# Two dot products of a graph kernel's tail: summed on ScalarE instead of VectorE

## The chip, the cores and the metric

The kernel runs on one core of a Trainium2 chip. A core has TensorE (PE: matrix products into PSUM), VectorE (DVE), ScalarE (ACT: functions of one operand, with an optional running sum of what it writes), GpSimd (POOL) and SyncE (SP, which here issues the DMAs between device memory and SBUF). Each engine works through its own queue in order and waits on semaphores for the others. The metric is the device time of one execution in microseconds; lower is better.

## The reference, cut to what matters

There are 32 graphs of 512 nodes with 64 features. Four layers follow each other, each with a residual and a norm over the features: a degree-normalised product with the adjacency matrix, a Chebyshev convolution of order 4, an attention in hyperbolic space (logarithm map, sigmoid attention, exponential map, projection), and an aggregation by weighted quantiles over a thinned neighbourhood, with a small two-layer network behind it. The change touches the end of the third layer. There the sum over neighbours becomes the tangent vector `u` of each node, and this is mapped back to the ball:

```python
def mobius_add(x, y, c):
    x2 = jnp.sum(x * x, axis=-1, keepdims=True)
    y2 = jnp.sum(y * y, axis=-1, keepdims=True)
    xy = jnp.sum(x * y, axis=-1, keepdims=True)
    num = (1.0 + 2.0 * c * xy + c * y2) * x + (1.0 - c * x2) * y
    den = 1.0 + 2.0 * c * xy + c * c * x2 * y2
    return num / jnp.maximum(den, MIN_NORM)
...
support_t = jnp.einsum('bij,bijd->bid', att, x_local)
support_t = jnp.clip(support_t, -CLAMP, CLAMP)
return proj(expmap(support_t, x, c), c)
```

The kernel never forms the pairwise vectors. It needs two dot products per node over the 64 features: of `x` with the weighted sum `S` of the neighbours (for the coefficient of `x` in `u`), and of `u` with `x` (the `xy` of the Moebius sum).

## The kernel before

A graph is a batch. Its 512 nodes lie as 128 partitions by T = 4 groups, a node's 64 features along the free dimension, so a `wide` tile is 128x4x64 and a `col` tile, one number per node, 128x4. Each batch passes through stages that the code calls lanes:

- `front` (L1000) loads the adjacency matrix and the features and does the first two layers. Its result, with some columns of scalars, goes to `FLS` (L1564), a tile with two halves: batch b uses half b % 2 (L1076).
- `pairs` (L1086) forms the 512x512 attention in float32 on TensorE, ScalarE and VectorE, and ends in `SS`, the weighted sums, copied from PSUM.
- `tail` (from L1211, still in that function) is the mapping back. The first dot product (`q`, tile `tail_xs`, L1215) enters `s1`; `v = x * s1` and `u = S * hb - v` follow, clipped. Then come the square sum `un` (L1224) and the second dot product `ux` (L1225). A long run of 128x4 operations, mostly on GpSimd, with one tanh on ScalarE, turns `un` and `ux` into two coefficients; `ux` is first read at L1238, after the tanh. The last reader of the batch's half of `FLS` is `scaled(v, x2, al)` (L1259). A layer norm gives `x3`.
- `graph` thins the neighbourhood and ranks the nodes by neighbour count. `gather` (L1270) selects neighbours by one-hot products on TensorE, into the strips `SB` and `SH`. `sort` (L1368) and `head` (L1399, once for two batches) run sorting networks of VectorE minima and maxima over them and weigh the quantiles (`sort_prod`, `PRS`). `finish` and `dense` (L1444 on) do the small network and store the result.

`rowsum` (L847) is used for the two dot products alone. It multiplies on VectorE into the tile `pr` and sums with one reduction of 128x256 to 128x4. `square` (L855) does its sums otherwise: four ScalarE activations of 128x64, one for each group, that write a throwaway tile `junk` (one buffer for each lane) and accumulate into one column of the result. The hardware executes each of these as an ACTIVATE and an ACTIVATION_READ_ACCUMULATOR.

What sets the order is a planner, the class `Order`. While the lanes are called, batch by batch, `op` (L289) only records each operation with its engine, an assumed issue time, an assumed latency and its dependences. `issue` (L361) then lays all operations of all batches out over five simulated queues and emits them in that order, which the hardware queues keep. Two things steer it:

- due times: `due` (L334) gives every operation a time, period x (batch + a number from `STAGES`), the number read off the lane's list of five knots by how deep the operation lies in its lane. The period is 80. Of the operations that are ready on an engine the planner takes the one with the earliest due time.
- margins: `after` (L354) says when a result can be used. On another engine that is the end plus the latency plus `HOP` (0.05) plus `LATE` (0.08).

Where the planner sees TensorE idle for more than 0.3, it puts in fillers (L453), products that keep the engine active: on zeros, or, while no accumulation is open, on constants.

Of the kernel before, what the change touches and what calls it, by code (L numbers as in the profile page):

```python
# [8 lines left out]
F32 = mybir.dt.float32  # L9
# [5 lines left out]
AF = mybir.ActivationFunctionType  # L15
OP = mybir.AluOpType
# [4 lines left out]
P = 128  # L21
# [218 lines left out]
class Order:  # L240
# [3 lines left out]

    ENGINES = ("PE", "DVE", "ACT", "POOL", "SP")
    HOP = 0.05
    LATE = 0.08
    STAY = 58.8

    def __init__(self, nc, tc):  # L250
# [103 lines left out]
    def after(self, d, i, end, full):  # L354

        a, b = self.ops[d], self.ops[i]
        if a[0] == b[0]:
            return end + (a[2] if full and a[0] != "PE" else 0.0)
        return end + a[2] + self.HOP + self.LATE

# [109 lines left out]
def tile_adj_resnorm(ctx: ExitStack, tc: tile.TileContext, x, adj, nodemask, w1k, b1k, att_w, att_b,  # L470
                     w1, b1, w2, b2, out):
    nc = tc.nc
    B, N, D = x.shape
    T = N // P
# [12 lines left out]
    pools = {}  # L487
# [3 lines left out]
    seq = Order(nc, tc)  # L491

    def width(a):
        n = 1
        for d in a.ap[1:]:
            n *= d[1]
        return n

    def vec(f, out, ins, one=False, scalars=(), reads=None, **kw):

        n = width(reads if reads is not None else out)
        tiles = [out] + list(ins)
        rate = 1.04e-3
        if not any(a.space == PSUM for a in tiles):
            half = all(a.dtype in (F16, BF16) for a in tiles)
            if one:
                rate = 0.26e-3 if half else 0.52e-3
            elif half:
                rate = 0.52e-3
        sc = [a for a in scalars if isinstance(a, bass.AP)]  # L510
        seq.op("DVE", 0.07 + n * rate + 0.065 * len(sc), 0.085, f, [out], list(ins) + sc)

    def tt(out, a, b, op):
        vec(lambda: nc.vector.tensor_tensor(out, a, b, op=op), out, [a, b])  # L514
# [14 lines left out]
    def reduce(out, a, op):  # L529
        vec(lambda: nc.vector.tensor_reduce(out, a, axis=AX.X, op=op), out, [a], reads=a)  # L530
# [12 lines left out]
    def act(out, a, f, bias=None, scale=1.0, accum_out=None, after=None):  # L543
        sc = [x for x in (bias, scale) if isinstance(x, bass.AP)]
        kw = {k: v for k, v in (("bias", bias), ("accum_out", accum_out)) if v is not None}
        n = width(out)
        table = "exp" if f in (AF.Ln, AF.Exp) else "sig" if f in (AF.Sigmoid, AF.Tanh) else None
        near = 0.06 if a.space == PSUM else 0.1
        seq.op("ACT", near + n * 0.83e-3 + 0.09 * len(sc) + (0.09 if accum_out is not None else 0.0),
             0.1, lambda: nc.scalar.activation(out, a, f, scale=scale, **kw), [out, accum_out], [a, after] + sc, table)  # L550
# [247 lines left out]
    def col(name):  # L798
        return seq.tile(pools["small"], [P, T], F32, name, 2)

    def wide(name, tag=None):
        return seq.tile(pools["small"], [P, T, D], F32, name, 1, tag)
# [44 lines left out]
    def rowsum(a, b, name):  # L847

        pr = wide("pr")
        tt(pr, a, b, op=OP.mult)  # L850
        s = col(name)
        reduce(s, pr, OP.add)
        return s

    def square(a, name):  # L855
# [230 lines left out]
    def pairs(b, res):  # L1086
# [126 lines left out]
        s1 = col("s1")  # L1213
        gtt(s1, SS[:, :, D], SS[:, :, D + 1], op=OP.add)
        q = rowsum(x2, S, "xs")  # L1215
        stt(s1, q, -2.0, s1, op0=OP.mult, op1=OP.add)
        tt(s1, s1, hh, op=OP.mult)
# [5 lines left out]
        ts(u, u, 1e6, -1e6, op0=OP.min, op1=OP.max)  # L1223
        un = square(u, "un")  # L1224
        ux = rowsum(u, x2, "ux")  # L1225
        uc = col("uc")
        gts(uc, un, TINY * TINY, None, op0=OP.max)
# [277 lines left out]
    def within_bounds():  # L1505

        gm, BT = pools["gm"], B * T
        seq.lane = "graph"
        p1, p2, p3 = bank(), bank(), bank()
        ge = [seq.tile(gm, [P, T, N], F16, "ge", 1, t).rearrange("p t n -> p (t n)") for t in ("nbT", "v")]  # L1510
        ge = [ge[s % 2][:, s // 2 * BT:(s // 2 + 1) * BT] for s in range(K + 1)]
        seq.lane = "check"
        m = M3.rearrange("p b t -> p (b t)")

        for s in range(K + 1):
            ts(ge[s], m, float(s), None, op0=OP.is_gt)
        for s in range(K + 1):
            mm(p1[:BT, s:s + 1], ge[s], onesP[:, 0:1], start=True, stop=True)
        cs = seq.tile(gm, [BT, K + 1], F16, "cs")
        act(cs, p1[:BT, :K + 1], AF.Copy)  # L1520
        mm(p2[:B, :K + 1], graphs[:BT, :], cs, start=True, stop=True)
        off = seq.tile(gm, [B, 2, K + 1], F16, "off")
        for i, op in enumerate((OP.is_gt, OP.is_lt)):
            tt(off[:, i, :], p2[:B, :K + 1], limits[:, i, :], op=op)
        bad = seq.tile(gm, [B, 1], F32, "bad")
        reduce(bad, off.rearrange("p i s -> p (i s)"), OP.max)
        badh = seq.tile(gm, [B, 1], F16, "badh")
        cp(badh, bad)
        mm(p3[:1, 0:1], badh, onesP[:B, 0:1], start=True, stop=True)
        ts(flag, p3[:1, 0:1], 0.0, None, op0=OP.is_gt)  # L1530
# [2 lines left out]

    STAGES = {"front": (-0.67, -0.59, -0.59, -0.4, -0.35), "pairs": (1.01, 1.02, 1.54, 1.44, 1.34),
              "tail": (2.23, 2.13, 2.56, 2.68, 2.58), "graph": (0.84, 1.06, 1.03, 1.48, 2.2),
              "gather": (2.92, 2.89, 2.92, 3.03, 2.93), "sort": (4.18, 4.47, 4.53, 5.09, 6.03),
              "head": (4.54, 5.59, 5.59, 6, 7.54), "ends": (4.04, 4.143, 4.245, 4.348, 4.45),
              "check": (1.75, 1.83, 1.91, 1.99, 2.07)}  # L1540

# [1 line left out]
    with ExitStack() as fast:  # L1543
# [59 lines left out]
        within_bounds()  # L1603
        seq.issue(80.0, STAGES, stay_active, 0.3)
        seq.lane = "dense"
# [141 lines left out]
    with tc.If(flagv > 0):  # L1747
        with ExitStack() as slow:
# [24 lines left out]
            for h in range(4):  # L1773
                t = cst.tile([P, T, QC * ROWS], BF16, name=f"parts{h}")
# [32 lines left out]
def build(inputs):  # L1807
    import numpy as np
    import concourse.bacc as bacc

    nc = bacc.Bacc("TRN2", target_bir_lowering=False, num_devices=1)
    arrays, args = {}, []
    for name in _INS:
        a = np.ascontiguousarray(inputs[name])
        if a.dtype == np.bool_:
            a = a.view(np.uint8)
        arrays[f"in_{name}_dram"] = a
        args.append(nc.dram_tensor(f"in_{name}_dram", a.shape, mybir.dt.from_np(a.dtype), kind="ExternalInput").ap())
    args.append(nc.dram_tensor("out_0_dram", inputs["x"].shape, F32, kind="ExternalOutput").ap())
    with tile.TileContext(nc) as tc:  # L1820
        tile_adj_resnorm(tc, *args)
    return nc, arrays
# [8 lines left out]
```

## Time and profile before

| | us |
|---|---|
| median of 3 runs | 2337.36 (2331.5 to 2339.77) |
| the profiled execution | 2326.41 |
| its span, first to last instruction | 2324.6 |
| reductions of the two dot products (`tail_xs`, `tail_ux`) on VectorE | 64, 13.1 + 13.1 busy |
| products before them (`tail_pr`) on VectorE | 64, 13.3 + 13.3 busy |
| accumulating squares of the tail (`tail_junk<-tail_u`) on ScalarE | 128, 33.9 busy, and 26.4 for the accumulator reads |
| table loads on ScalarE | 126 profiled, 1.283 each |

The busy time of an engine counts each moment once. In a group of instructions, though, the single times are added, and neighbours on VectorE and ScalarE overlap: the next one starts before the one before it has ended. What an instruction costs its engine is therefore read from the distance between two starts. A busy TensorE is not TensorE at its peak. The profile names instructions by the tile that is written, with the lane in front: `tail_junk<-tail_u` is the square of `u` in the lane `tail`. As helpers record all operations, many instructions share one line (L514 for all products of two tensors, L550 for all activations), and the tiles tell them apart.

### The profile page before, as it was taken

To read this page: it belongs to the slowest core of one execution; us is meant where nothing else is said; L and a number is where in the kernel's file an instruction comes from. 1 tells how busy PE (TensorE), PEld (TensorE's weight loads), DVE (VectorE), ACT (ScalarE), POOL (GpSimd) and SP (SyncE) were. 2 spreads that over 40 slices of the span, in tenths; PEclk is the share of its full clock that TensorE was granted. 3 is DMA by queue.
4 is the path that set the end of the run, shared out by engine and by line. 5 is a ranking of instruction groups with operands and counts; after the bars stand their busy time and mean duration, and the time that the engine had idled before them with its cause. 6 is when DMAs were issued, how large, how long until landed. Compare 5 with 4: busy or idle time off the path is not lost. (4 is left out here: it accounts for less than half of the span.)

```text
span 2324.6 us, 53396 instructions
## 1 busy us (share of the span) xinstructions
PE 2177.0 (94%) x18555; PEld 1504.3 (65%) x18555; DVE 2115.8 (91%) x6952; ACT 2033.9 (87%) x5818; POOL 1098.7 (47%) x2256
## 2 busy tenths in 40 slices
PE   6999999999999999999999999999999999999987
PEld 4666666666666666666666666666666666666655
DVE  4556999999999999999999999999999999999996
ACT  6798989999998989898989989898998989899753
POOL 1133445545464544545445554544555454454431
PEclk9999999999999999999999999999999999999999
DMA  1010001111000110100011111001111000100000
GB/s 45 21 42 12 18 22 31 27 28 31 27 18 21 34 28 26 33 26 20 22 31 28 27 33 26 19 21 32 29 27 33 26 19 17 29 15 8 13 15 14
DMA packets 131716, 57.72 MB, mean 25 GB/s; under 512 B 56140, under 2 KB 129516, under 8 KB 131436
## 3 DMA queue, kind: packets, MB, share of 16 engines
q1 hardware_dynamic: 126432, 50.09, 8.0%
q0 software_dynamic: 3840, 3.94, 0.8%
q8 instruction: 148, 2.42, 0.4%
q14 instruction: 132, 1.08, 0.2%
q10 hardware_dynamic: 1164, 0.18, 0.0%
HBM read 41.86 MB, written 12.32 MB: 23 GB/s over the span
## 5 line engine op out<-in xcount | busy, mean ns | idle before, releaser
L514 DVE TENSOR_TENSOR SB<-SB 128x92 f32<-128x92 f32 (+12 forms) x1312 | 555.3, 448 | 15.3 <-ACT SB L550 6.2
L569 PE MATMUL gather_bank<-gather_oh,tail_x3h 128*64 128x256 f16 (+5 forms) x5376 | 496.5, 318 | 7.4 <-ACT SB L550 7.1
L569 PEld LDWEIGHTS <-tail_x3h 128*64 128x64 bf16 x5376 | 333.9, 110 | 134.4 <-issue 26.2
L569 PE MATMUL pairs_bank<-pairs_FT 67*128 67x512 f32 (+7 forms) x768 | 305.6, 504 | 8.5 <-DVE pairs_L L521 2.7
L518 DVE TENSOR_SCALAR gather_oh<-graph_slot 128x256 f16<-128x256 f16 (+9 forms) x864 | 252.7, 343 | 27.1 <-PE gather_bank L569 23.5
L514 DVE TENSOR_TENSOR SH<-SH 128x288 f32<-128x288 f32 (+18 forms) x880 | 271.2, 342 | 3.8
L569 PE MATMUL front_bank<-front_AT,front_y 128*64 128x256 f32 x1536 | 190.4, 385 | 12.3 <-DVE front_y L514 11.5
L569 PEld LDWEIGHTS pairs_bank<-pairs_FT 67*128 67x128 f32 (+1 forms) x768 | 127.7, 190 | 83.8 <-issue 18.2
L582 POOL DMA_INDIRECT tail_x<-ranked,graph_spot x120 | 136.5, 1137 | 74.5 <-issue 41.4
L569 PEld LDWEIGHTS <-graph_nbT 128*128 128x128 f16 x1536 | 117.4, 98 | 78.3 <-issue 34.2
L569 PEld LDWEIGHTS front_bank<-front_AT,front_y 128*64 128x64 f32 x1536 | 108.1, 137 | 78.1 <-DVE front_y L514 22.2
L813 POOL TENSOR_TENSOR front_rs<-front_var,mhalf 128x4 f32<-128x4 f32 x64 | 81.1, 1267 | 131.4 <-DVE front_var L518 120.2
L569 PE MATMUL graph_bank<-graph_perm,graph_V 128*128 128x512 f16 x512 | 137.4, 379 | 5.3 <-DVE graph_perm L518 2.7
L569 PE MATMUL pairs_bank<-FLS,pairs_Wt 128*128 128x66 f32 x1024 | 125.6, 273 | 0.3
L514 DVE TENSOR_TENSOR pairs_RW<-pairs_RW,pairs_EX 128x640 f32<-128x640 f32 x128 | 104.7, 818 | 22.9 <-ACT pairs_EX L550 14.6
L569 PEld LDWEIGHTS pairs_bank<-FLS,pairs_Wt 128*128 128x128 f32 x1024 | 121.0, 192 | 2.5 <-DVE pairs_Wt L521 1.7
L569 PEld LDWEIGHTS <-tabs 128*128 128x128 f16 x1296 | 84.0, 98 | 48.3 <-issue 17.4
L550 ACT ACTIVATE graph_junk<-graph_bank,graph_keyh 128x512 f16<-128x512 f32 x128 | 88.0, 688 | 21.8 <-PE graph_bank L574 18.0
L569 PE MATMUL graph_bank<-UC,graph_nbT 128*128 128x512 f16 (+3 forms) x512 | 97.5, 303 | 8.4 <-ACT graph_v L550 4.1
L550 ACT ACTIVATE SB<-gather_bank 128x448 f32<-128x448 f32 (+7 forms) x288 | 89.3, 359 | 18.2 <-PE gather_bank L569 11.9
L569 PE MATMUL PA<-identf,sort_prod 128*96 128x128 f32 (+3 forms) x576 | 103.0, 282 | 1.5 <-DVE sort_prod L514 1.5
L541 POOL TENSOR_SCALAR tail_uc<-tail_un 128x4 f32<-128x4 f32 x32 | 20.7, 646 | 176.6 <-ACT tail_junk L550 170.9
(374 smaller groups left out, 6469.5 us busy)
## 6 DMA issues: line engine op xcount, KB each, us to landing
front_A<-in_adj_dram SPq DMA_DIRECT2D x128, 256.0 KB, 2.9
front_xr<-in_x_dram SPq DMA_DIRECT2D x32, 128.0 KB, 2.2
xs<-tail_x SPq DMA_DIRECT2D x32, 128.0 KB, 2.1
out_dram<-head_zo SPq DMA_DIRECT2D x31, 128.0 KB, 2.0
ranked<-sort_ap SPq DMA_DIRECT2D x30, 128.0 KB, 1.9
tail_x<-ranked,graph_spot POOLq DMA_INDIRECT x120, 2.5
out_dram<-tail_ends SPq DMA_DIRECT2D x1, 128.0 KB, 1.9
wk<-in_L_gnn_weight_dram ACTq DMA_DIRECT2D x1, 64.0 KB, 3.3
```

The lines of the kernel that those rows point to most:

```text
L514: vec(lambda: nc.vector.tensor_tensor(out, a, b, op=op), out, [a, b])
L518: vec(lambda: nc.vector.tensor_scalar(out, a, s1, s2, op0=op0, **kw), out, [a], True, (s1, s2))
L541: gp(lambda: nc.gpsimd.tensor_scalar(out, a, s1, s2, op0=op0, **kw), out, [a] + [x for x in (s1, s2) if isinstance(x, bass.AP)])
L550: 0.1, lambda: nc.scalar.activation(out, a, f, scale=scale, **kw), [out, accum_out], [a, after] + sc, table)
L569: return nc.tensor.matmul(out, w, a, start=start, stop=stop)
L582: seq.op("POOL", 1.15, 2.0, lambda: nc.gpsimd.indirect_dma_start(out, None, rows, bass.IndirectOffsetOnAxis(ap=at, axis=0)), [out], [at], ...
L813: seq.op("POOL", 1.6, 0.5, lambda: nc.gpsimd.tensor_tensor(y, v, mhalf, op=OP.pow), [y], [v])
```

## The change

`rowsum` still multiplies on VectorE. The sum over the features is no longer one reduction on VectorE: four copies on ScalarE, one per group of nodes, each write the throwaway tile and accumulate into one column of the result. Four numbers that steer the planner change with it: the margin `LATE`, and three knots of the due times, in the lanes `front`, `tail` and `sort`. All other code is the same; since the planner lays everything out anew, the order of instructions differs on all engines.

```diff
     HOP = 0.05
-    LATE = 0.08
+    LATE = 0.101
...
         pr = wide("pr")
         tt(pr, a, b, op=OP.mult)
         s = col(name)
-        reduce(s, pr, OP.add)
+        for t in range(T):
+            act(seq.tile(pools["small"], [P, D], F32, "junk"), pr[:, t, :], AF.Copy, accum_out=s[:, t:t + 1])
         return s
...
-    STAGES = {"front": (-0.67, -0.59, -0.59, -0.4, -0.35), "pairs": (1.01, 1.02, 1.54, 1.44, 1.34),
-              "tail": (2.23, 2.13, 2.56, 2.68, 2.58), "graph": (0.84, 1.06, 1.03, 1.48, 2.2),
-              "gather": (2.92, 2.89, 2.92, 3.03, 2.93), "sort": (4.18, 4.47, 4.53, 5.09, 6.03),
+    STAGES = {"front": (-0.67, -0.59, -0.59, -0.4, -0.39), "pairs": (1.01, 1.02, 1.54, 1.44, 1.34),
+              "tail": (2.23, 2.13, 2.55, 2.68, 2.58), "graph": (0.84, 1.06, 1.03, 1.48, 2.2),
+              "gather": (2.92, 2.89, 2.92, 3.03, 2.93), "sort": (4.18, 4.47, 4.53, 5.09, 5.8),
```

## The prediction

> **What bounds the kernel now.** I read the page's busy shares first, then its slices, then the windows of the level stretch, then the waits of VectorE, and last the rows of the instructions that change.
>
> ```profile
> PE 2177.0 (94%) x18555; PEld 1504.3 (65%) x18555; DVE 2115.8 (91%) x6952; ACT 2033.9 (87%) x5818; POOL 1098.7 (47%) x2256
> ...
> DVE  4556999999999999999999999999999999999996
> ACT  6798989999998989898989989898998989899753
> ```
>
> No engine stands alone. VectorE starts late and then stays full to the end; ScalarE has holes and falls off early. The level stretch says it more sharply:
>
> ```profile
> 500.00:1700.00 1200.00, 1143.99 (x9844) 790.93 (x9843) 1149.89 (x3750) 1100.69 (x3178) 621.83 (x1211) 1.00 0.10 27
> ```
>
> Over 1200 us VectorE is busy 95.8% (third number pair), TensorE 95.3%, ScalarE 91.7%. ScalarE has 99.3 us to spare, VectorE 50.1, TensorE 56.0. The granted clock is 1.00, so the clock is no part of this.
>
> ```profile
> DVE gather_oh L518 <- PE gather_bank L569: 23.5, 22, 4.0
> DVE front_q L514 <- PE front_bank L574: 15.6, 6, 5.1
> DVE graph_v L518 <- ACT graph_v L550: 14.8, 13, 4.3
> DVE pairs_RW L514 <- ACT pairs_EX L550: 14.6, 16, 2.2
> ...
> DVE front_var L518 <- ACT front_junk L550: 8.0, 9, 3.5
> ```
>
> What idle time VectorE has is split between TensorE and ScalarE. The page's chain of waits breaks off at the last instruction, so I walked back by its rule (to what released an instruction, or else to the one before it on its engine) from the last TensorE instruction before 2200 us. Between 500 and 1700 us this path passes 676.6 us through VectorE, 307.2 through ScalarE, 153.1 through TensorE, 39.8 through GpSimd, the rest hops. So 676.6 / 1149.9 = 0.588 of VectorE's busy time lies on the path, and 307.2 / 1100.7 = 0.279 of ScalarE's. These are my exchange rates.
>
> **The change part by part.**
>
> *The reductions that go.* In the timeline an instruction's price is the distance from its start to the next start, as neighbours overlap.
>
> ```profile
> 1063.52 0.40 DVE L530 TENSOR_REDUCE tail_ux<-tail_pr 128x4 f32<-128x256 f32 x1
> 1063.84 0.20 DVE L514 TENSOR_TENSOR PRS<-PRS 128x64 f32<-128x64 f32 x1
> ```
>
> That distance has a median of 0.329 us over the 64 reductions (two per batch, 32 batches): VectorE loses 64 x 0.329 = 21.1 us. On the path: 21.1 x 0.588 = 12.4 us.
>
> *The copies that come.* Each reduction becomes four accumulating copies of 128x64, 256 in all. The nearest rows are the accumulating squares of the same tail:
>
> ```profile
> 1067.65 0.28 ACT L550 ACTIVATE tail_junk<-tail_u 128x64 f32<-128x64 f32 x1
> 1067.79 0.23 ACT L550 ACTIVATION_READ_ACCUMULATOR tail_junk<-tail_u 128x1 f32 x1
> 1067.89 0.37 ACT L550 ACTIVATE XA<-front_xr,front_shift 128x63 f32<-128x63 f32 x1
> 1068.12 0.28 ACT L550 ACTIVATE tail_junk<-tail_u 128x64 f32<-128x64 f32 x1
> 1068.27 0.23 ACT L550 ACTIVATION_READ_ACCUMULATOR tail_junk<-tail_u 128x1 f32 x1
> 1068.53 0.26 ACT L550 ACTIVATE tail_junk<-tail_u 128x64 f32<-128x64 f32 x1
> ```
>
> Followed by other work, such a pair holds ScalarE for 0.24 us (1067.65 to 1067.89; median of 107: 0.239). Followed by its like it waits for the one scratch buffer: 0.41 here, median of 21: 0.381. So between 61 and 98 us. In the changed kernel's order 243 copies are followed by other work and 13 by a copy: 243 x 0.239 + 13 x 0.381 = 63.0 us. One of 127 table loads (1.283 us) goes: +61.7 us. On the path at the old rate: 61.7 x 0.279 = +17.2 us.
>
> Here a page of the Trainium skill differs from the row. "ScalarE: Activation LUTs", section "What ACT_TABLE_LOAD costs", gives an ACTIVATE with immediate operands 186 ns plus 0.833 ns per element, less some 93 ns of overlap with its neighbour; it prices no reading of the accumulator. My estimate from it is 146 ns a copy, 37 us in all, 10 us on the path, and the sum would fall below zero. The row has the accumulator read in it and decides.
>
> *The exchange.* At the old rates: 17.2 - 12.4 = +4.8 us. But the rates move. The stretch holds 17.7 batches (67.7 us from batch to batch). ScalarE gains 17.7 x 61.7 / 32 = 34 us and comes to 94.6%; VectorE loses 17.7 x 0.66 = 12 us and comes to 94.8%. Equally loaded, they would share the path, (0.588 + 0.279) / 2 = 0.434 each: 61.7 x 0.434 - 21.1 x 0.434 = +17.6 us. I take the middle, +11 us, as the new load sits between the old picture and a third engine, TensorE, just as full. Both ends stay in the range.
>
> *The new wait.* `tail_s` now waits for ScalarE where its summand came from its own engine. Behind it on VectorE stands a sorting step (`SB<-SB`) in 17 of 32 cases and the head's products in 9, and behind those TensorE's transposes of `sort_prod`. The nearest row is `front_var` waiting for `front_junk`: 8.0 us over 32 batches, 4.7 on the path. The order puts 9 to 48 VectorE instructions between product and use (median 23, before 4), so I take 0, with 4.7 as the other end. `tail_ux` is read by GpSimd only after `tail_th`, some 12 us later; that covers its copies.
>
> *A longer tail.* In ScalarE's order the way from `pairs_SS` to the last `tail_v<-FLS,tail_al` grows from 100.8 to 118.1 instructions (mean of batches 8 to 25). Eight are the new copies (8 x 0.239 = 1.9 us); 9.3 are others, at 41.6 us / 100.8 = 0.41 us each, 3.8 us. The tail gets about 5.7 us longer. That `tail_v` is the last reader of its `FLS` half, which the front two batches on overwrites; from its end to that write the trace has 7.1 to 17.1 us in four batches of six, 2.5 and 1.5 in the others. I take 0, as the order moves other work into the gap; the other end is the second rival's.
>
> *The rest.* The order has 679 fillers on zeros for 591, and 100 for 114 of the other kind, 74 more at 0.273 us, most in the last stretch:
>
> ```profile
> 2260.00:2325.00 65.00, 46.71 (x369) 34.52 (x365) 42.24 (x131) 19.57 (x79) 12.87 (x12) 0.90 0.06 14
> ```
>
> TensorE idles there 18 us of 65 and hides them; without that cover 74 x 0.273 = 20 us. GpSimd's 2329 and SP's 298 instructions are the same ones, no DMA is added. In the last batch the result of the first dot product comes 11 VectorE instructions after its product instead of 3, at about 0.27 us each: at most 2.2 us, which the sorting of earlier batches covers (VectorE is busy 59.4 of 60 us from 2200 on); I take 0. The new margin and due times reorder everything a little. Bounds for that: two batches took 134.0 to 138.2 us, on average 135.6, so eleven such steps all at the fastest would give -18 us, all at the slowest +29. I take 0.
>
> Sum against the profiled execution: it took 2326.4 us (span 2324.6). 2326.4 + 11 = 2337.4. The median of the runs shown, 2337.4, lies 11 us above the profiled one, so the forecast in their terms is 2348 us.
>
> **The rivals.**
>
> *VectorE alone sets the pace, and the copies fall into ScalarE's holes: faster.* For it: VectorE has the highest share and a path share twice ScalarE's; ScalarE has 99 us of holes in the stretch and needs 34; nearly all copies have other work next to them. Against it: ScalarE's waits are for results (`graph_junk` for TensorE 18 us, `pairs_RW` for VectorE 17.5), and work put before them pushes them. Price: 12.4 to 21.1 us gained, 17 in the middle: 2320 us.
>
> *The tail runs into the two halves of FLS: clearly slower.* Once the tail is longer than the gap, `FLS` of batch b+2 waits, with its pairs stage behind it. At 5.7 us longer the gaps 2.5 and 1.5 are exceeded by 3.2 and 4.2 us, two batches in six: 7.4 / 6 x 24 level batches = 30 us, with +4.8: 2337 + 35 = 2372 us. It decides from 1.5 us of lengthening on. For it: in the new order that gap shrinks from 19.9 to 7.9 ScalarE instructions. Against it: in the old one the write follows its own `front_rs` by 1 to 3 us, so it was not what the front waited for.
>
> *Gain and cost cancel:* at the old rates and with small gains of order, -5 to +5 us: 2337 us.
>
> **How the numbers follow.** Forecast 0.35, VectorE's pace 0.31, FLS 0.17, cancelling 0.17. Less than 0.3% (7 us) can't be told from no change here. Faster: 0.31 and a little of the forecast, 0.33. Same: 0.17 and the forecast's lower edge, 0.20. Slower: the rest, 0.47. The forecast's own range is 2342 to 2355; with the other cases and the bounds of order the range is 2316 to 2376.
>
> **What would show it.** Right: copies at 0.24 us to the next start, ScalarE 94 to 95% busy in the level stretch, VectorE one point lower, 0.3 to 0.5 us more per batch. VectorE's pace: batch distance below 67.4 us, and ScalarE's waits shorter by what the copies take. FLS: the gap between `tail_v<-FLS,tail_al` and the next write of that half near zero in many batches, with batch distances up by a microsecond. The forecast is wrong if TensorE turns out to carry the path, for then neither exchange rate holds, or if the reordering outweighs both.

## The result, and the profile after

The changed kernel takes 2354.58 us (median of 5 runs, 2350.01 to 2360.37), the kernel before 2336.94 us beside it (5 runs). The ratio is 1.0086, 95% interval 1.0057 to 1.0114. Slower was forecast, at 2348 us: a price of 11 us was expected, 17.6 us lie between the medians. The profiled execution took 2350.0 us, its span is 2348.2.

The busy line and two rows of the slices, from the page after:

```profile
span 2348.2 us, 53979 instructions
...
PE 2192.0 (93%) x18604; PEld 1522.8 (65%) x18629; DVE 2093.9 (89%) x6888; ACT 2083.5 (89%) x6329; POOL 1076.9 (46%) x2256
...
DVE  4556899999989999998999989899999999899896
ACT  6798998999989999999999999899998999998743
```

VectorE is 21.9 us less busy than before (2115.8 to 2093.9), ScalarE 49.6 us more, and the span is 23.6 us longer. So VectorE's idle time grew by 45.5 us, twice what the reductions had cost it. ScalarE's idle time shrank by 26.0 us: about half of its new work fell into holes. In the slices VectorE's row, all nines in the middle before, now has eights.

The level stretch, in the windows of after:

```profile
500.00:1700.00 1200.00, 1139.91 (x9739) 789.30 (x9754) 1130.84 (x3683) 1121.89 (x3442) 591.27 (x1196) 0.99 0.10 27
```

VectorE 94.2% (95.8 before), ScalarE 93.5% (91.7), TensorE 95.0% (95.3). The two loads have come together nearly as computed: ScalarE stays half a point below the 94 to 95% forecast, and VectorE fell by 1.6 points where one was said. TensorE, which received no work there, is a little less busy. VectorE's waits after:

```profile
DVE gather_oh L518 <- PE gather_bank L569: 47.5, 34, 6.7
DVE pairs_RW L514 <- ACT pairs_EX L550: 18.8, 15, 2.7
DVE pairs_RW L514 <- ACT pairs_RW L550: 18.6, 13, 4.8
DVE graph_v L518 <- ACT graph_v L550: 18.0, 17, 4.2
...
DVE front_var L518 <- ACT front_junk L550: 6.8, 3, 3.4
```

The second of the two waits in the pairs stage was, before:

```profile
DVE pairs_RW L514 <- ACT pairs_RW L550: 8.2, 13, 1.8
```

The wait for the gather's matmuls doubled (23.5 to 47.5 us), and those for ScalarE in the pairs stage grew by 4 and 10 us. Nothing in this list waits for the new copies. They stand, with the squares, in the answer for the tile `tail_junk`:

```profile
L550 ACT ACTIVATE tail_junk<-tail_pr x256: 238/254/346, 115.4 to 2235.7; 128x64 f32<-128x64 f32 x128
L550 ACT ACTIVATION_READ_ACCUMULATOR tail_junk<-tail_pr x256: 185/194/292, 115.5 to 2235.9; 128x1 f32 x128
...
  POOL tail_uc L541: 166.5, 30
  PEld front_bank L574: 3.2, 9
  PEld pairs_bank L569: 1.1, 4
  POOL tail_xy L537: 0.3, 1
```

256 copies with their accumulator reads (minimum, median and maximum in ns). From one start to the next start it is 0.239 us where other work follows and 0.380 where a copy follows, as priced. The last lines say who waited for the tile: GpSimd's `tail_uc` waits for the squares, as before (170.9 us); no VectorE instruction waits.

Batch by batch, the distance between the first ScalarE writes to `FLS`, from batch 8 to batch 26, went from 67.74 to 68.66 us, 0.9 more where 0.3 to 0.5 had been said. The way from `pairs_SS` to the last `tail_v<-FLS,tail_al` went from 41.6 to 45.9 us, 4.3 more where 5.7 had been said.

### The profile page after: what moved, and what is told of

It reads as the page before. It is cut to its first block, busy times and chain, and to the rows that moved or that the text cites. A ratio compares the mean times of both kernels' runs of the same rounds, so it can differ in the third digit from the quotient of the medians.

```text
span 2348.2 us, 53979 instructions
## 1 busy us (share of the span) xinstructions
PE 2192.0 (93%) x18604; PEld 1522.8 (65%) x18629; DVE 2093.9 (89%) x6888; ACT 2083.5 (89%) x6329; POOL 1076.9 (46%) x2256
## 4 chain that ended last, share of the span: by engine, by line
DVE 56%; ACT 22%; PE 14%; POOL 3%; issue 3%; DMA 1%; ACTq 0%; POOLq 0%; DVEq 0%
DVE SB L514 15%; DVE SH L514 8%; DVE gather_oh L518 5%; PE gather_bank L569 4%; ACT pairs_RW L550 4%; DVE pairs_Q L514 3%; PE front_bank L569 3%; DVE pairs_Wt L521 3%; DVE pairs_L L521 3%; ACT pairs_EX L550 2%; PE pairs_bank L569 2%; PE graph_bank L569 2%; DVE pairs_RW L514 2%; DVE sort_prod L514 2%; DVE pairs_EX L521 1%
## 5 line engine op out<-in xcount | busy, mean ns | idle before, releaser
L569 PE MATMUL pairs_bank<-pairs_FT 67*128 67x512 f32 (+7 forms) x768 | 313.6, 512 | 6.1 <-DVE pairs_L L521 3.0
L518 DVE TENSOR_SCALAR gather_oh<-graph_slot 128x256 f16<-128x256 f16 (+9 forms) x864 | 256.3, 344 | 47.9 <-PE gather_bank L569 47.5
L813 POOL TENSOR_TENSOR front_rs<-front_var,mhalf 128x4 f32<-128x4 f32 x64 | 93.3, 1459 | 158.9 <-DVE front_var L518 134.1
L569 PE MATMUL graph_bank<-graph_VP,UC 128*128 128x512 f16 x320 | 90.7, 379 | 9.4 <-ACT graph_slot L550 8.1
```

The lines of the kernel that those rows point to most:

```text
L518: vec(lambda: nc.vector.tensor_scalar(out, a, s1, s2, op0=op0, **kw), out, [a], True, (s1, s2))
L569: return nc.tensor.matmul(out, w, a, start=start, stop=stop)
L813: seq.op("POOL", 1.6, 0.5, lambda: nc.gpsimd.tensor_tensor(y, v, mhalf, op=OP.pow), [y], [v])
```

## The experiments

Twelve runs in three groups. All ratios are against the kernel before on the same chip in the same group; us are the ratio times its median there (2360.48, 2332.92 and 2330.65 us). The three chips differ, and the first in a way that matters: see the last section. Its numbers were therefore taken again where the reading rests on them.

### First group: numbers apart from copies, and the load apart from the order

`copies_old_plan` is the kernel before with the copies alone; the planner lays it out with the old margin and due times. `reduce_new_plan` is its counterpart: the reductions with the new numbers.

```diff
 copies_old_plan, against before
-        reduce(s, pr, OP.add)
+        for t in range(T):
+            act(seq.tile(pools["small"], [P, D], F32, "junk"), pr[:, t, :], AF.Copy, accum_out=s[:, t:t + 1])
 reduce_new_plan, against before: LATE and STAGES of after
```

> The copies on ScalarE, with the margin LATE and the due times of the kernel before. If the copies themselves cost the time (load on ScalarE, longer tail): 10 to 20 us over the kernel before, 2347 to 2357 us, as in the changed kernel. If the four new planner numbers cost it: within 7 us of 2337 us. If those numbers mend a part: over 2357 us.

> The reductions on VectorE, with the margin LATE and the due times of the changed kernel. If the copies cost the time: within 7 us of 2337 us. If the planner numbers cost it: 2347 us or more.

Measured: the copies with the old numbers 1.0159 (1.0131 to 1.0187), +38 us. The reductions with the new numbers 1.0130 (1.0104 to 1.0156), +31 us. Both corners are worse than the changed kernel's 1.0086. The new numbers are no improvement by themselves; they help only with the copies. The reductions with the new numbers also ran at the lowest mean granted clock of the group, 0.978 against 0.986 for before, so a part of their 31 us may go with the clock.

A kernel that is laid out anew mixes the load with the order. `act_load` and `both_loads` therefore keep the order of before. Extra instructions ride behind a planned one at set distances, unknown to the planner. In `both_loads` a copy of one column, 128x4, stands in the place of each reduction; it leaves out the two dot products, so it shows times and computes something else.

```diff
 act_load, against before
-        reduce(s, pr, OP.add)
+        i = reduce(s, pr, OP.add)
+        for t in range(T):
+            seq.riders.setdefault(i, []).append((0.5 + 0.8 * t, "ACT", lambda t=t: nc.scalar.activation(
+                JK, pr[:, t, :], AF.Copy, accum_out=JA[:, t:t + 1])))
 both_loads, against act_load
-        i = reduce(s, pr, OP.add)
+        i = vec(lambda: nc.vector.tensor_copy(s, pr[:, :, 0]), s, [pr], reads=pr)
```

> The kernel before in its own order; behind each reduction ScalarE gets four more accumulating copies of the product, whose sums nobody reads (256 in all, 63 us of ScalarE, nothing waits for them). Load theory with path shares: 63 x 0.279 to 63 x 0.434, 17 to 27 us slower, 2354 to 2364 us. If the copies fall into ScalarE's holes: at most 5 us slower.

> As the run with the unread copies, and each reduction is replaced by a copy of 128x4 on VectorE in its place (the dot products are left out: the column holds one product), so VectorE loses 64 x 0.26 = 16 us; order kept, tail not longer. Load theory: 17 to 27 us less 16 x 0.588 to 16 x 0.434, so 8 to 20 us slower than before, 2345 to 2357 us. If the longer tail or the new order is what costs the time: no slower than before, 2325 to 2340 us.

Measured: `act_load` 1.0150 (1.0122 to 1.0179), +35 us; `both_loads` 1.0138 (1.0112 to 1.0165), +33 us. Both cost more than expected. And relieving VectorE of the reductions gave back 3 us, with intervals that overlap, where 7 to 9 were expected.

### Second group: VectorE's side alone, FLS, and the clock

`after_again` is the changed kernel. `after_fls3` gives `FLS` three slots, with the slots folded to two in the planner's bookkeeping so that the order stays. `dve_unload` is before with the column copy in place of the reduction and nothing on ScalarE; it too leaves out the dot products. `after_fill` puts more fillers into TensorE's planned gaps.

```diff
 after_fls3, against after
-        FL = FLS[:, b % 2]
+        FL = FLS[:, b % 3]
 dve_unload, against before
-        reduce(s, pr, OP.add)
+        vec(lambda: nc.vector.tensor_copy(s, pr[:, :, 0]), s, [pr], reads=pr)
 after_fill, against after
-        seq.issue(80.0, STAGES, stay_active, 0.3)
+        seq.issue(80.0, STAGES, stay_active, 0.1)
```

> The changed kernel once more, on the chip of this group's other runs, so that they have a partner. Theory A (the exchange of loads costs some 30 us and the new planner numbers give a part of it back) and every other expect the ratio of the first measurement, 1.006 to 1.011. Should the ratio be near 1.016, what the old plan with the copies gave in the first group, then the planner numbers give nothing back.

> The changed kernel with its order of instructions kept, and with three slots of FLS in place of two, so that a batch's SS waits for the sum of the batch three before it and not two. Rival 2 of the prediction (the longer tail is held by the two halves): 8 to 25 us faster than the changed kernel of this group. Theory A (a write still follows its own front_rs, and the slot is free by then): within 4 us of the changed kernel.

> The kernel before with its order of instructions kept, and each of the 64 reductions replaced by a 128x4 copy of one column on VectorE, so that the two dot products are left out and nothing goes to ScalarE. It takes some 64 x (0.329 - 0.09) = 15 us from VectorE alone. The prediction's step (0.588 of it on the path, or 0.4 to 0.6 by the rates that it weighed): 6 to 9 us faster than before. Theory A (the path moves to ScalarE and TensorE, as the runs with both loads had it): 0 to 4 us faster.

> The changed kernel with the order of its working instructions kept, and with some 208 more fillers on TensorE (a gap of 0.21 us in the plan is filled, where it was 0.41 us). Clock theory (0.007 of granted clock lost is some 10 us of the change's price): the granted clock goes up from 0.987 and the time down by about 1.5 us for each 0.001, if the fillers lie in the windows that lose it. Load theory (the clock is a symptom): the same time within 4 us, or up to 20 us slower where fillers stand before work that is due.

Measured: `after_again` 1.0085 (1.0071 to 1.0099), +20 us, as the first time. `after_fls3` 1.0105 (1.0087 to 1.0122), 4.5 us over `after_again` by the medians: the two slots were not what held it. `after_fill` 1.0076 (1.0062 to 1.0090), the same as `after_again`; its mean granted clock over six runs is 0.9868, that of `after_again` 0.9867. The fillers neither raised the clock nor cost anything.

`dve_unload` 0.9957 (0.9941 to 0.9973), −10 us (−6 to −14). The column copy takes 0.072 us to the next start, so 64 x (0.329 − 0.072) = 16.4 us were taken from VectorE; the old path rate would give 9.7 us. The 0 to 4 us of theory A are excluded.

### Third group: the loads again on another chip, and half a dose

Between the first two groups stood a contradiction: unloading VectorE is worth 10 us alone and nothing under ScalarE's load. Either it is so, or the first chip made it so. `act_half` is `act_load` with two copies of four.

```diff
 act_half, against act_load
-        for t in range(T):
+        for t in range(0, T, 2):
```

> The kernel of act_load once more. In the first group's profiles TensorE's completions stop 13 to 17 times for 1 to 5 us (30 to 46 us in all), in the second group's and in that of before once. Theory L (the stops belong to those kernels): the ratio of act_load comes back at 1.012 to 1.018, with the stops. Theory C (they belong to the chip of the first group, on which before took 1% longer too): on a chip without them the four copies behind each reduction cost what the prediction's two rates gave, 17 to 27 us, 1.007 to 1.012, or less.

> act_load with two of the four unread copies behind each reduction, some 31 us of ScalarE in place of 62, all else in the order of before. If ScalarE's time is paid by a rate, half of what act_load costs in this group (8 to 17 us). If the first microseconds fall into idle time and only the later ones count, under a third of it.

> The kernel of both_loads once more: act_load with the reductions replaced by a 128x4 copy, so that the dot products are left out. The second group gave the unloading of VectorE alone 9 us. If the two loads add, 9 us under act_load of this group. If the path has moved to ScalarE once it is loaded (as the first group had it, 3 us under), 0 to 4 us under.

> The copies with the planner numbers of before, once more. Theory N (the new numbers give back about half of what the copies cost): 1.013 to 1.019, against the 1.0085 that the changed kernel gave twice. Theory C (the first group's chip made it dear): 1.005 to 1.011, so that the new numbers are worth nothing that can be told.

Measured:

| kernel | ratio | interval | us against before | us per batch, 8 to 26 |
|---|---|---|---|---|
| `act_half` | 1.0041 | 1.0026 to 1.0056 | +10 | 68.18 |
| `act_load_again` | 1.0108 | 1.0087 to 1.0129 | +25 | 68.89 |
| `both_loads_again` | 1.0132 | 1.0108 to 1.0155 | +31 | 68.80 |
| `copies_old_again` | 1.0172 | 1.0146 to 1.0197 | +40 | 68.73 |

So Theory C holds for `act_load`, whose price is now 25 us, within the 17 to 27 of the prediction's rates, and fails for `copies_old_again`, which is as dear as on the first chip. And `both_loads_again` is not 9 us under `act_load_again` but 6 above, with intervals that overlap: the relief is worth nothing that can be told here, on two chips. Some of the 6 may go with the clock, whose mean was 0.991 in `both_loads_again` and 0.994 in `act_load_again`.

What the dose does is read from the windows of the level stretch, first `dve_unload`:

```profile
500.00:1700.00 1200.00, 1146.83 (x9863) 791.92 (x9869) 1144.73 (x3754) 1104.71 (x3186) 617.17 (x1216) 1.00 0.10 27
```

`act_half`:

```profile
500.00:1700.00 1200.00, 1141.47 (x9765) 784.09 (x9773) 1144.91 (x3727) 1110.42 (x3303) 595.00 (x1196) 0.99 0.10 27
```

`act_load_again`:

```profile
500.00:1700.00 1200.00, 1127.64 (x9671) 776.83 (x9678) 1135.16 (x3692) 1115.28 (x3409) 597.09 (x1188) 1.00 0.10 27
```

`both_loads_again`:

```profile
500.00:1700.00 1200.00, 1129.14 (x9680) 778.52 (x9687) 1128.97 (x3694) 1115.31 (x3414) 592.96 (x1188) 1.00 0.10 27
```

From before (1100.7) over half to the full load, ScalarE is busy 1110.4 and 1115.3 us of 1200, and TensorE falls from 1144.0 over 1141.5 to 1127.6: less is done in the same time. Between the last two rows only VectorE's busy time moves, by 6.2 us; ScalarE's and TensorE's stay within 1.5. The time freed on VectorE became idle time on VectorE. The chain of waits on the pages, over the whole span, shows a shift. `dve_unload`:

```profile
DVE 52%; ACT 23%; PE 19%; POOL 3%; issue 2%; DMA 0%; POOLq 0%; ACTq 0%; DVEq 0%
```

`act_half`:

```profile
DVE 52%; ACT 30%; PE 13%; POOL 2%; issue 2%; DMA 0%; POOLq 0%; ACTq 0%; DVEq 0%
```

`act_load_again`:

```profile
DVE 45%; ACT 37%; PE 13%; POOL 3%; issue 2%; DMA 0%; ACTq 0%; POOLq 0%; DVEq 0%
```

ScalarE's part of the chain grows from 23% over 30 to 37% as it is loaded, VectorE's falls from 52 to 45. The first half of the copies costs 10 us, the second half 16 (25.2 − 9.6): here the price of a copy rose with the load on its engine, though 10 still lies in the 8 to 17 us that a fixed rate was expected to give. The shift alone does not explain the missing relief. With 45% of the chain still on VectorE, 16.4 us less work there would be worth some 7 us by that share, and nothing came.

The kernels that the planner laid out with the copies look different. The changed kernel, `after`:

```profile
DVE 56%; ACT 22%; PE 14%; POOL 3%; issue 3%; DMA 1%; ACTq 0%; POOLq 0%; DVEq 0%
```

`copies_old_again`:

```profile
DVE 53%; ACT 26%; PE 14%; POOL 4%; issue 2%; DMA 0%; POOLq 0%; ACTq 0%; DVEq 0%
```

The walk back that the prediction made for before, done the same way between 500 and 1700 us, passes 696 us through VectorE and 305 through ScalarE in the changed kernel. Before it was 677 and 307; in `act_load_again` it is 512 and 479. So the chain moves to ScalarE with the unread copies in the kept order, and not where the planner has placed the copies.

## Why the prediction was right in sign, and where its sum was wrong

**The prices of the instructions were right.** 0.239 us per copy followed by other work, 0.380 followed by its like, 243 and 13 of them: measured as said. The one row that had the accumulator read in it decided rightly against the page "ScalarE: Activation LUTs" of the Trainium skill, section "What ACT_TABLE_LOAD costs", from which 146 ns was the estimate: by that estimate the sum would have fallen below zero.

**What failed is the step "The exchange"**, in the sentence "Equally loaded, they would share the path, (0.588 + 0.279) / 2 = 0.434 each: 61.7 x 0.434 - 21.1 x 0.434 = +17.6 us". The premise did not come: in the changed kernel the two engines are loaded nearly alike, 94.2 and 93.5%, and the same walk gives 696 / 1130.8 = 0.616 of VectorE's busy time and 305 / 1121.9 = 0.272 of ScalarE's, close to the rates of before. By these rates the exchange would cost 61.7 x 0.272 - 21.1 x 0.616 = +4 us; 17.6 and 20 were measured. Neither the old shares nor equal ones price this change, and that the upper end, 17.6, equals the first measurement is chance.

With the order kept, the two products can be tested singly. The first was right: 61.7 x 0.434 = 26.8 us for the copies, measured 25 (20 to 30). The second was not. 21.1 x 0.434 = 9.2 us were booked as gain; with the unread copies there, the runs show none: +6 us on one chip, −3 on the other, with intervals that overlap both times. VectorE's relief alone is worth 10 us in `dve_unload`, as its old rate has it. So gain and loss, each about right alone, did not add: in the kept order the exchange costs 31 us and not 11 or 17.6. This holds for one placement of the unread copies; no other was tried. Whether VectorE's relief is also worth nothing in the changed kernel's own order was not tested.

**What brought the forecast near is the step taken at 0, "The rest", and that is luck.** "The new margin and due times reorder everything a little ... I take 0", with bounds of −18 and +29 us. Reordering moved much. Laid out by the planner with the old numbers the copies cost 40 us (34 to 46), 9 more than with the kept order; with the new numbers 20 (17 to 23). So the new numbers are worth 20 us to this kernel, and against the kept order the reordering gives 11. These come from different chips, each against its own kernel before. Counted in this way, the changed kernel's 20 us are 31 of exchange less 11 of order: the forecast had the exchange 20 us too small and did not book the 11. This is a difference between kernels; it does not show a cause for each part.

Where the time lies can be read from the first ScalarE write to `FLS` in batches 8 and 26 of the profiled executions:

| kernel | to batch 8, us | batch 8 to 26 | from there to the end |
|---|---|---|---|
| before | 557.7 | 1219.4 | 547.5 |
| `after` | 558.4 | 1235.8 | 554.0 |
| `copies_old_again` | 578.9 | 1237.1 | 554.3 |
| `both_loads_again` | 565.1 | 1238.4 | 556.0 |

The new numbers gain 20.5 us on the old ones before batch 8, and 1.3 us in the eighteen batches after it; batch 8 comes at 558.6 us in `after_again` and at 579.6 in `copies_old_plan`, on other chips. So they make a better start; from batch 8 to 26 the three kernels with the copies are 16 to 19 us behind, 0.9 to 1.1 us per batch, in whichever order.

**The new wait: 0, right.** No VectorE instruction waits for the copies.

**The longer tail: size nearly right, price 0, right.** 4.3 us longer for 5.7 said. The mean distance to the next write of the slot shrank from 7.8 to 3.7 us. Some slices even interleave, as −6.2 us shows at the lowest. Still a third slot gave nothing: a write goes on following its own `front_rs` by 0.2 to 3.5 us, which was the argument against that rival.

**The fillers: 0, right.** 208 more of them changed nothing.

**The rivals.** VectorE alone does not set the pace: the copies would have to fall into ScalarE's holes for that, and even half of them cost 10 us. FLS fell with `after_fls3`. Cancelling, −5 to +5 us, lies outside the interval of both measurements (13 to 27 and 17 to 23 us).

**The clock.** "The clock is no part of this" holds for the level stretch of before and not quite for after: the mean granted clock is 0.994 before and 0.987 after in the first profiles, 0.9901 and 0.9867 as means over the second group's runs. Within one kernel's runs there, the time falls by 1.1 to 2.0 us for each 0.001 of clock, so some 4 to 7 of the 20 us may go with the clock. That is an estimate; the run meant to test it did not move the clock. That unread copies cost time without a loss of clock is shown by `act_load_again`, which is 25 us slower at a mean clock of 0.994, while before had 0.991 in that group.

What stays open: what the old numbers lose in the first eight batches, and by which path the copies cost 16 us in the level stretch although the shares of the chain hardly moved. The profile shows in the changed kernel a doubled wait of `gather_oh` for TensorE (47.5 us; 39.2 in `copies_old_again`), and no single wait that the new numbers removed. Nor is there a version here that computes the two sums and beats the kernel before. The 10 us of `dve_unload` are what a free place for the two sums would be worth, and ScalarE is no such place: half of the copies already cost that much.

## What to carry to other kernels

A share of the chain of waits, read from one profile, is an estimate of a price and has to be tested: here two engines loaded alike did not share the chain alike, and 16 us taken from VectorE were worth 10 us alone and nothing beside ScalarE's load. So when work moves between two nearly full engines, price the load, and count the relief as zero at the slower end of the range. In a kernel that a planner lays out, separate load from order by adding unread instructions to the kept order, and compare the times at the same batches: the planner's new numbers were worth 20 us here, as much as the whole change, and nearly all of it in the first eight of 32 batches.

## What the runs showed of the hardware

**TensorE's clock was halved after windows that were only partly empty.** Windows of after, four neighbours of 3.4 us (busy time and instructions of TensorE, weight loads, VectorE, ScalarE and GpSimd, then the granted clock):

```profile
1339.25:1342.66 3.41, 3.41 (x18) 1.54 (x15) 2.69 (x9) 2.54 (x13) 3.12 (x1) 1.00 0.17 38
1342.66:1346.08 3.42, 1.48 (x13) 0.77 (x13) 3.17 (x14) 3.04 (x10) 0.89 (x4) 1.00 0.00 0
1346.08:1349.50 3.42, 3.42 (x20) 1.89 (x18) 1.71 (x6) 2.28 (x9) 1.67 (x4) 0.50 0.28 81
1349.50:1352.90 3.40, 3.40 (x29) 2.07 (x25) 1.40 (x3) 3.38 (x11) 2.07 (x2) 1.00 0.04 10
```

TensorE was busy 1.48 of 3.42 us, the next window ran at 0.50, and full clock came back after it. The trace of before has 5 such dips, that of after 11. In the 3.4 us ahead of them TensorE was busy for some 0.4 to 0.8 of the time, but for two: 0.72 of 3.41 us near the end of before, and 0.00 of 3.41 us at 2175.5 us of after. Not every window so empty is followed by a dip. The Trainium skill, "TensorE: Matmul & The Clock Gate", Part 1, says that half clock comes after an idle window of about 3.4 us. The length agrees; of these sixteen windows only one was idle.

**One chip showed stops that the others did not.** The first group's chip ran the kernel before 28 us slower than the second's (2360.48 for 2332.92). In all four profiles taken there, TensorE's completions stop more than a dozen times for 1 to 5 us, some 140 us apart, 30 to 50 us together. In the other ten profiles there is at most one, of 3 to 4 us. Such a stop in the timeline of `act_load` on that chip:

```profile
1257.74 0.21 PE L574 MATMUL graph_bank<-onesP,graph_nbT 128*128 128x1 f16 x3
...
1258.32 0.27 PE L579 MATMUL head_bank<-identf,tail_x 128*128 128x128 f32 x1
...
1262.03 0.16 DVE L523 TENSOR_SCALAR graph_mi<-graph_bank 128x4 int32<-128x4 f32 x1 [6.03 <-remote]
...
1262.06 0.35 ACT L555 ACTIVATE SB<-gather_bank 128x214 f32<-128x214 f32 x1 [2.94 <-remote]
...
1262.31 1.07 PE L574 MATMUL graph_bank<-UC,graph_nbT 128*128 128x512 f16 x4 [3.73 <-DVE graph_do L526]
```

And the same place in the same kernel on the third group's chip:

```profile
1248.17 0.21 PE L574 MATMUL graph_bank<-onesP,graph_nbT 128*128 128x1 f16 x3
...
1248.42 0.16 DVE L523 TENSOR_SCALAR graph_mi<-graph_bank 128x4 int32<-128x4 f32 x1 [2.00 <-PE gather_bank L574]
```

The matmuls of `graph_bank` are on record at 1257.7 us, but VectorE and ScalarE, which wait for TensorE's results, go on only at 1262.03 and 1262.06, when the trace has four of TensorE's signals within 0.12 us. "remote" is what the profile writes where no instruction ends near the signal. On the other chip VectorE goes on 0.25 us after the matmuls started. What stops TensorE there was not found. The kernel before was not profiled on that chip, so that the stops are also what made it 28 us slower there is likely and not shown. The ratios of the other kernels against it there were near those elsewhere in two cases (38 and 40 us, 33 and 31) and not in one (35 and 25); `reduce_new_plan` was run there alone, and its 31 us carry that doubt.
